# Two graph-attention layers: r stored by target tile, and the neighbour lists' parts regrouped so that an adjacency load has rows of 4 KB

## The chip, the cores and the metric

One of the eight cores of a Trainium2 chip runs the whole program in one launch. The metric is device time in microseconds (us): the median of several executions of the same program, less being better. The profile shows one further execution, recorded instruction by instruction, with its own time.

## The reference: what is computed

`x` is 4096 nodes by 256 features, `adj` a 4096 x 4096 matrix of 0 and 1 in int32 (a node pair is joined with a probability of about 0.8%, and each node is joined to itself). Two attention layers run one after the other over the same matrix. Cut to what matters:

```python
# layer 0: 8 heads of 128; layer 1: 4 heads of 64, with W and a of its own
Wh  = einsum('nf,hfd->hnd', x, W_heads)
s1, s2 = Wh @ a1, Wh @ a2                       # one number per node and head
e   = leaky_relu(s1[target] + s2[source], 0.2)  # for each pair
att = softmax(where(adj > 0, e, -inf), over sources)
hp  = att @ Wh
# layer 0: x = layernorm(x + elu(hp) @ W_out + b_out)
# layer 1: x = layernorm(x + hp), the result
```

`exp(leaky_relu(a + b))` is the larger of two products, each of a factor of the target and a factor of the source. So the kernel needs, per node and head, one factor of the target, called `r`, and two of the source, called `c` and `q`.

## The kernel before, in words

**Layer 0 is sparse.** The 4096 targets form 32 tiles of 128, and each tile 8 groups of 16, so there are 256 groups. For a group the kernel lists all nodes that are joined to any of its 16 targets, and fetches the table rows of these nodes by an indirect DMA (a gather, line 858): four gathers of 128 rows for a group. A table row holds the 256 features, the source's factors, and one 16-bit word per group of the phase, which tells which targets the source is joined to. VectorE makes the weights from `r` and the row's factors (lines 964 to 978), TensorE multiplies weights and rows (line 986), and the sums are turned into features, projected and normalised (from line 1025 on).

**The lists come from bit words.** Work runs in 8 phases of 4 tiles (512 targets). For each phase the adjacency rows of its targets are loaded in 16 pieces of 128 targets by 1024 sources (`load`, line 538, its DMA at line 548), turned into bf16 (`convert`), and multiplied on TensorE by powers of two (`count`), which leaves one word per source and group. The words lie in a tile of 128 partitions by 1024 columns: partition block `q` of 32 partitions (one per group) and its 1024 columns are the list's part `q`, which is a quarter of the nodes. Before the change part `q` is the nodes 1024q to 1024q + 1023. The words arrive in two halves of 512 columns, [...]and so a piece for one half takes, for two of the parts, 512 sources each: two runs of 2 KB in a row of the adjacency. From the words and the node's number (`node`, written once at line 458) VectorE picks the largest eight at a time (`take`), at most 160 in each part. The words also go into the table's rows by way of four transposes and copies (`bits`, `note`), and `publish` (line 676) writes them to the table in DRAM.

**r goes through DRAM.** The factor `r` of the targets is made in 4 chunks of 8 tiles (`Scores.chunk`), transposed to one row of 128 values per head and tile, and stored in the DRAM tensor `r_d` (`store`, line 423, its DMA at line 426). Before the change `r_d` of a chunk is laid out as head, tile, target. `Near` (line 909) then loads, for each target tile, the 8 heads' rows of that tile into all 128 partitions (`rb`, line 916): eight runs of 512 B for each partition, 1024 runs in all. Right behind it on the same queue `Near` loads the tile's own table rows (`own`, line 920). Layer 1 has its own `r_d`; it reads, for one head, the 8 tiles of a chunk in a run of 4 KB (line 1272).

**What sets the order.** The layer 0 code stands in one order written out by hand (`tc.manual_schedule`), and each engine works through its own list in that order:
- SyncE's queue (SP) issues nearly all plain loads: the adjacency pieces, `rb`, `own`, `y`, the weights, and `table` stores of later phases. An instruction that waits there holds all that stand behind it.
- ScalarE (ACT) has a queue too: half of the first phase's adjacency pieces, the layer 0 weights `w0T` (line 774), the stores of `r_d`, and the four `table` stores of the first phase (line 678).
- GpSimd (POOL) issues the gathers. `gather` (line 852) runs 5 groups ahead, with 6 buffers.
- Adjacency pieces of later phases have 3 buffers, and a piece is converted two pieces after it is loaded. A planner (`pick`, `busy`, `spare`) spreads VectorE's list work over the groups; its costs are not touched by the change.

**The opening** (`opening`, line 766) is all that stands before the first gather: the first phase's adjacency, the factors, the first phase's lists, the table's first copy, and the second phase's adjacency. After it the loop over the 256 groups begins (line 1189). **Layer 1** (from line 1378) is dense: it loads the transposed adjacency in pieces with rows of 4 KB (line 1279), makes weights on VectorE and multiplies on TensorE.

If a list overflows or a factor leaves its range, a flag at the end (line 1448) starts a slow general path. It does not run with these inputs.

Of the kernel before, what the change touches and what calls it, by code (L numbers as in the profile page):

```python
# [9 lines left out]
F32 = mybir.dt.float32  # L10
BF16 = mybir.dt.bfloat16
I32 = mybir.dt.int32
# [6 lines left out]
P = 128  # L19
# [243 lines left out]
def fast_path(  # L263
# [72 lines left out]
    class Scores:  # L336
# [3 lines left out]
        def __init__(self, n, H, pj, cj):  # L340
            self.n, self.H, self.pj, self.cj = n, H, pj, cj
            self.v = small.tile([P, KC, 2, H], F32, tag="v", name=f"v_{n}", bufs=1)
            self.d = const.tile([P, NT, H], F32, name=f"d_{n}")
            self.mx = const.tile([P, H], F32, name=f"mx_{n}")
            self.r_d = dram.tile([NCH, H, CT, P], F32, name=f"r_d_{n}")

        def weights(self, a_sb, wT_sb):
            pv = ps_m.tile([P, KC, 2, self.H], F32, tag="m", name=f"pv_{self.n}")
# [11 lines left out]
        def chunk(self, k, src):  # L360

            n, H = self.n, self.H
            held = {}

            def scores():
                ps = held["ps"] = ps_0.tile([P, CT, 2, H], F32, tag="o1", name=f"ps_{n}_{k}")
                for t in range(CT):
                    for c in range(KC):
                        nc.tensor.matmul(  # L369
                            ps[:, t],  # L370
                            src[:, c, ts(k * CT + t, P)],
                            self.v[:, c],
                            start=(c == 0),
                            stop=(c == KC - 1),
                        )

            def pull():
                pc = held["pc"] = small.tile(
                    [P, CT, 2, H], F32, tag="pc", name=f"pc_{n}_{k}", bufs=2
                )  # L380
                nc.vector.tensor_copy(pc, held["ps"])
                if k == 0:
                    ext = small.tile([P, H], F32, tag="ext", name=f"ext_{n}", bufs=1)
                    nc.vector.tensor_reduce(
                        ext, pc.rearrange("p t a h -> p a h t")[:, 1], AX.X, ALU.max
                    )
                    held["pe"] = ps_m.tile([H, P], F32, tag="m", name=f"pe_{n}")
                    nc.tensor.transpose(held["pe"], ext, ident)

            def top():  # L390

                if k == 0:
                    top = small.tile([H, 1], F32, tag="top", name=f"top_{n}", bufs=1)
                    nc.vector.tensor_reduce(top, held["pe"], AX.X, ALU.max)
                    dg = small.tile([H, H], F32, tag="dg", name=f"dg_{n}", bufs=1)
                    nc.vector.tensor_scalar(dg, ident[0:H, 0:H], top, None, ALU.mult)
                    held["pm"] = ps_m.tile([P, H], F32, tag="m", name=f"pm_{n}")
                    nc.tensor.matmul(held["pm"], ones[0:H, :], dg, start=True, stop=True)

            def factors():  # L400
                if k == 0:
                    nc.vector.tensor_copy(self.mx, held["pm"])
                pc = held["pc"]
                mx = self.mx.unsqueeze(1).to_broadcast([P, CT, H])
                r = held["r"] = small.tile([P, H, CT], F32, tag="r", name=f"r_{n}_{k}", bufs=1)
                rt = r.rearrange("p h t -> p t h")
                nc.vector.tensor_tensor(rt, pc[:, :, 0], mx, ALU.add)
                nc.vector.tensor_scalar(r, r, SPREAD, None, ALU.min)
                nc.scalar.activation(r, r, AF.Exp, scale=1.0 - SLOPE)
                d = self.d[:, ts(k, CT), :]  # L410
                nc.vector.tensor_tensor(d, pc[:, :, 1], mx, ALU.subtract)
                dc = small.tile([P, CT, H], F32, tag="dc", name=f"dc_{n}_{k}", bufs=1)
                nc.vector.tensor_scalar(dc, d, -SPREAD, RISE, ALU.max, ALU.min)
                nc.scalar.activation(
                    self.pj[:, ts(k, CT), :], dc, AF.Exp, scale=SLOPE - (0.0 if n == 0 else 1.0)
                )
                nc.scalar.activation(self.cj[:, ts(k, CT), :], dc, AF.Exp)

            def turn():
                held["pr"] = ps_m.tile([H * CT, P], F32, tag="m", name=f"pr_{n}_{k}")  # L420
                nc.tensor.transpose(held["pr"], held["r"].rearrange("p h t -> p (h t)"), ident)

            def store():
                row = small.tile([H * CT, P], F32, tag="row", name=f"row_{n}_{k}", bufs=1)
                nc.vector.tensor_copy(row, held["pr"])
                nc.scalar.dma_start(self.r_d[k].rearrange("h t p -> (h t) p"), row)

            return [scores, pull, top, factors, turn, store]

# [26 lines left out]
    node = keep0.tile([P, QN], mybir.dt.uint16, name="node")  # L456
    for q in range(NQ0):
        nc.gpsimd.iota(
            node[ts(q, GP), :], pattern=[[-1, QN]], base=N - q * QN, channel_multiplier=0
        )  # L460
    one = const.tile([P, T], I32, name="one")
    nc.gpsimd.memset(one, 1)
# [67 lines left out]
    def words_of(s):  # L530

        pw = []
        raw, bins = {}, {}
        HN = QN // 2
        NW = PT * NQ0
        PQ = NQ0 // 2

        def load(m):

            k, t, q = m // (PT * PQ), m // PQ % PT, m % PQ  # L540
            if s == 0:
                G = gpool.tile([P, NB, RW], F32, tag="G", name=f"Ga_{m}")
                v = G.rearrange("p b w -> p (b w)")[:, 0 : 2 * HN].bitcast(I32)
                raw[m] = v.rearrange("p (a n) -> p a n", a=2)
            else:
                raw[m] = apool.tile([P, 2, HN], I32, tag="aq", name=f"aq_{s}_{m}")
            queue = nc.scalar if s == 0 and m % 2 else nc.sync
            queue.dma_start(
                raw[m],
                adj[ts(s * PT + t, P), :].rearrange("p (q k n) -> p k q n", k=2, n=HN)[  # L550
                    :, k, ts(q, 2)
                ],
            )

        def convert(m):
            mb = two.tile([P, 2, HN], BF16, tag="mb", name=f"mb_{s}_{m}", bufs=2)
            if s == 0:
                nc.vector.tensor_scalar(mb, raw.pop(m), 0.0, 0.5, ALU.is_gt, ALU.subtract)
            else:
                nc.scalar.activation(mb, raw.pop(m), AF.Sign, bias=half[:, 0:1])  # L560
            bins[m] = mb

        def count(m):


            k, t, q = m // (PT * PQ), m // PQ % PT, m % PQ
            if t + q == 0:
                pw.append(ps_0.tile([P, HN], F32, tag="o2", name=f"pw_{s}_{k}", bufs=1))
            mb = bins.pop(m)
            for a in range(2):  # L570
                r = ts(2 * q + a, GP)
                nc.tensor.matmul(  # L572
                    pw[k][r, :],
                    word[:, t, :],
                    mb[:, a],
                    start=(t == 0),
                    stop=(t == PT - 1),
                    tile_position=(0, (2 * q + a) * GP),
                    skip_group_check=True,
                )  # L580
            if t == PT - 1 and q == PQ - 1:
                if k == 0:
                    words[s] = two.tile([P, QN], F32, tag="ws", name=f"ws_{s}", bufs=2)

                nc.scalar.activation(
                    words[s][:, ts(k, HN)],
                    pw[k],
                    AF.Identity,
                    bias=half[:, 1:2],
                    scale=1.0 if s == 0 else 0.5,  # L590
                )

        lag = 5 if s == 0 else 2

        def piece(m):
            for f, mm in ((load, m), (convert, m - lag), (count, m - lag - 1)):
                if 0 <= mm < NW:
                    f(mm)

        return [lambda m=m: piece(m) for m in range(NW + lag + 1)]  # L600

    def lists_of(s):
# [15 lines left out]

        def others():

            j0 = s * PT * P
            o = ws[ts(j0 // QN, GP), ds(j0 % QN, PT * P)]
            nc.vector.tensor_tensor(o, o, other[ts(j0 // QN, GP), :], ALU.mult)

        def halve(k):

# [41 lines left out]
            held[k] = pt  # L668

        def note(k):  # L670
            o = tail[:, :, WD - F :].bitcast(I32).rearrange("p (q k) g -> p k q g", q=NQ0)
            pt = held.pop(k)
            for q in range(NQ0):
                nc.scalar.copy(o[:, ts(k, 4), q], pt[:, :, q])

        def publish(k, n):
            t = NT // n
# [231 lines left out]
    class Near:  # L909
# [3 lines left out]
        def __init__(self, i):  # L913
            self.i = i
            self.rb = two.tile([P, H0, P], F32, tag="rb", name=f"rb_0_{i}")
            nc.sync.dma_start(
                self.rb, sc0.r_d[i // CT, :, i % CT, :].unsqueeze(0).to_broadcast([P, H0, P])
            )
            self.rows = two.tile([P, RW], F32, tag="own", name=f"own_{i}")
            nc.sync.dma_start(self.rows, table[i // PT % 2][ts(i, P), :])  # L920
# [575 lines left out]
```

## Time and profile before

| what | value |
|---|---|
| median of 3 runs | 2341.47 us (2330.23 to 2343.05) |
| the profiled execution | 2615.83 us, of which its span 2614.0 us |
| opening, span 0 to 124 us | first gather issued at 123.33 us |
| layer 0's loop, 124 to 1860 us | POOL is busy for 1051 us of it |
| layer 1, 1860 to 2614 us | PE is busy for 726 us of it |
| DMA packets | 229,332, of which 33,664 of 512 B and 32,768 of 2 KB |
| mean granted TensorE clock | 0.900 |

The page of the profile has six parts: busy time by engine; the span in 40 slices; the DMA queues; the chain of work that ended last, followed back from the end; groups of instructions by line and form, with the idle time before them; and the DMA issues. Engines are PE (TensorE), PEld (its weight loads), DVE (VectorE), ACT, POOL and SP. A waiting time is put down to the one that ended it. Queue q1 is SP's, q10 ACT's, and q0 that of POOL's gathers. The profiled execution took 274 us longer than the median of the runs, so a stretch of it can't be taken for a stretch of a timed run without a second thought.

### The profile page before, as it was taken

The numbers are of one execution on the slowest core, as the hardware profiler recorded it, in microseconds if no ns is written. First come the engines' busy times: TensorE is split into PE (matmuls) and PEld (weight loads), VectorE is DVE, ScalarE is ACT, GpSimd is POOL, SyncE is SP. The second block draws the span as 40 slices with busy tenths as digits, with TensorE's granted clock in tenths as the row PEclk, the third lists the DMA queues.
The fourth block names the chain that finished last, engine by engine and source line by source line (L and its number), as shares of the span: only waits on it lengthen the run. The fifth ranks groups of instructions, "written<-read, shape, count | busy, mean of one in ns | idle before, by whom it ended". The sixth has DMA issues, their size and how long they took to land.

```text
span 2614.0 us, 35749 instructions
## 1 busy us (share of the span) xinstructions
PE 2171.0 (83%) x12585; PEld 1302.0 (50%) x12585; DVE 1994.5 (76%) x4347; ACT 804.0 (31%) x1569; POOL 1087.6 (42%) x1158
## 2 busy tenths in 40 slices
PE   4357877887788887788878778878899999999997
PEld 3234555565565555556545556656553432324433
DVE  4358687777777787767767886666599799999997
ACT  1313323322322322332332222312343444434332
POOL 1066566565665666656556666664000000010110
PEclk9978888888888898888889888888999999999998
DMA  7968465556636746755554644543676566666653
GB/s 258 237 161 240 133 152 181 153 141 185 182 110 145 218 139 158 197 144 151 158 168 123 138 121 115 131 124 83 227 245 192 173 203 200 214 202 222 185 180 98
DMA packets 229332, 443.54 MB, mean 170 GB/s; under 512 B 60820, under 2 KB 125463, under 8 KB 229143
## 3 DMA queue, kind: packets, MB, share of 16 engines
q1 hardware_dynamic: 168790, 264.94, 34.3%
q0 software_dynamic: 52224, 169.97, 23.7%
q10 hardware_dynamic: 8128, 6.25, 0.8%
q8 instruction: 101, 1.65, 0.2%
q14 instruction: 89, 0.72, 0.1%
HBM read 426.04 MB, written 23.40 MB: 172 GB/s over the span
## 4 chain that ended last, share of the span: by engine, by line
PE 63%; another core or an unknown queue 12%; DVE 8%; ACT 6%; DMA 5%; issue 5%; POOL 1%; SPq 0%; DVEq 0%; ACTq 0%; POOLq 0%
PE po L986 26%; PE po L1298 16%; PE po L1310 8%; PE ph L1046 3%; PE py L1069 3%; PE pa L1017 2%; DMA G<-table,ids 2%; ACT mb L560 1%; ACT ag L1010 1%; ACT rb_s L885 1%; PE ps L369 1%; PE pw L572 1%; DVE e L964 1%; DVE e L970 1%
## 5 line engine op out<-in xcount | busy, mean ns | idle before, releaser
L858 POOL DMA_INDIRECT G<-table,ids x1024 | 979.2, 956 | 618.6 <-issue 262.5
L1408 DVE SCALAR_TENSOR_TENSOR e<-rb,pj,mb 128x1024 f32<-128x1024 f32 x512 | 631.0, 1279 | 48.3 <-PE po L1310 24.4
L986 PE MATMUL po<-G,e 128*128 128x257 f32 x2048 | 618.5, 454 | 20.5 <-DVE e L978 9.0
L1298 PE MATMUL po<-e,wh 128*32 128x512 f32 x4096 | 623.9, 594 | 8.5 <-DVE e L1408 5.8
L986 PEld LDWEIGHTS po<-G,e 128*128 128x128 f32 x2048 | 432.3, 222 | 187.7 <-issue 54.8
L1310 PE MATMUL po<-e,cj 128*32 128x512 f32 x2048 | 457.6, 592 | 0.0
L1280 ACT ACTIVATE mb<-aq 128x1024 bf16<-128x1024 int32 x256 | 271.0, 1058 | 411.8 <-DVE e L1408 348.2
L986 PE MATMUL po<-own,eo 128*128 128x257 f32 x512 | 185.8, 448 | 246.1 <-ACT ag L1010 191.4
L1020 ACT COPY aT<-pa 128x256 f32<-128x256 f32 x256 | 94.9, 371 | 872.7 <-remote 307.0
L1298 PEld LDWEIGHTS po<-e,wh 128*32 128x32 f32 x4096 | 202.8, 110 | 281.2 <-issue 174.5
L446 POOL TENSOR_TENSOR rstd<-rstd,neg_half 128x1 f32<-128x1 f32 x32 | 28.4, 891 | 726.7 <-DVE rstd L445 537.1
L986 PEld LDWEIGHTS po<-own,eo 128*128 128x128 f32 x512 | 85.9, 211 | 269.7 <-ACT ag L1010 207.0
L986 PE MATMUL po<-Gs,e_s 32*128 32x257 f32 x512 | 202.8, 479 | 18.3 <-DVE e_s L907 18.3
L1310 PEld LDWEIGHTS po<-e,cj 128*32 128x32 f32 x2048 | 127.5, 110 | 137.8 <-issue 103.9
L964 DVE TENSOR_TENSOR e<-rb,side 128x512 f32<-128x512 f32 x256 | 175.8, 687 | 9.3 <-issue 0.3
L970 DVE TENSOR_TENSOR e<-e,side 128x512 f32<-128x512 f32 x256 | 175.8, 687 | 8.9
L978 DVE TENSOR_TENSOR e<-e,side 128x512 f32<-128x512 f32 x256 | 175.7, 686 | 8.8
L1005 DVE TENSOR_SCALAR rd_all<-po 128x1 f32<-128x1 f32 x256 | 38.6, 151 | 180.7 <-PE po L986 131.7
L1046 PE MATMUL ph<-aT,w_sb 128*128 128x128 f32 x1024 | 154.7, 296 | 7.9 <-issue 7.5
L1046 PEld LDWEIGHTS ph<-aT,w_sb 128*128 128x128 f32 x1024 | 143.1, 208 | 23.8 <-issue 18.0
L1010 ACT ACTIVATE ag<-po,rd_all 128x256 f32<-128x256 f32 x256 | 120.5, 471 | 96.5 <-DVE rd_all L1006 55.0
L986 PEld LDWEIGHTS po<-Gs,e_s 32*128 32x128 f32 x512 | 84.5, 206 | 117.6 <-issue 98.6
(158 smaller groups left out, 2089.6 us busy)
## 6 DMA issues: line engine op xcount, KB each, us to landing
aq<-in_adjT SPq DMA_DIRECT2D x256, 512.0 KB
aq<-in_adj SPq DMA_DIRECT2D x112, 512.0 KB
rb<-r_d SPq DMA_DIRECT2D x48, 512.0 KB
G<-table,ids POOLq DMA_INDIRECT x1024
table<-in_x SPq DMA_DIRECT2D x8, 1024.0 KB
table<-tail SPq DMA_DIRECT2D x56, 98.0 KB
own<-table SPq DMA_DIRECT2D x32, 152.5 KB
Ga<-in_adj SPq DMA_DIRECT2D x8, 512.0 KB
```

Of the source, the lines that this page charges most:

```text
L858: nc.gpsimd.indirect_dma_start(out=G[:, b, :], out_offset=None, in_=table[s % 2][:, :], in_offset=bass.IndirectOffsetOnAxis(ap=lists[s][:, ...
L964: nc.vector.tensor_tensor(e, rb[:, :, ts(n % GT, T)].unsqueeze(1).to_broadcast(sh), f_p[:, :, 0:H0].unsqueeze(3).to_broadcast(sh), ALU.mult,)
L970: nc.vector.tensor_tensor(e, e, f_p[:, :, H0:].unsqueeze(3).to_broadcast(sh), ALU.max)
L978: nc.vector.tensor_tensor(e, e, nb_p.unsqueeze(2).to_broadcast(sh), ALU.mult)
L986: nc.tensor.matmul(po, w.rearrange("p h t -> p (h t)"), v[:, 0 : F + 1], start=first, **kw)
L1010: nc.scalar.activation(ag, po[:, 0:F], AF.Copy, scale=rd_all[:, n : n + 1])
L1020: nc.scalar.copy(aT[:, :, :, ts(n % GT, T)], pt)
L1046: nc.tensor.matmul(phs[k][:, hh, :], w_sb[:, c, ts(h, D0)], aT[:, c, h, :], start=(c == 0), stop=(c == KC - 1),)
L1280: nc.scalar.activation(mb, aq, AF.Relu, scale=OPEN)
L1298: nc.tensor.matmul(po[q][ts(b, DQ), :], wh[:, j, k, d : d + DQ], es[k][:, ts(q, HB)], start=(j == 0), stop=(j == NT - 1), tile_position=(0 ...
L1310: nc.tensor.matmul(po[NQ][r0 : r0 + DQ, :], sc1.cj[:, j, 2 * g + k : 2 * g + k + 1].to_broadcast([P, DQ]), es[k][:, ts(q, HB)], start=(j = ...
L1408: nc.vector.scalar_tensor_tensor(e, rb[k], sc1.pj[:, j, h : h + 1], mb, ALU.max, ALU.min)
```

## The change

Three things change together, and nothing else.

1. `r_d` of layer 0 is laid out as tile, head, target. `store` writes its 64 rows of 512 B to permuted places, and `Near` reads one run of 4 KB for each partition, 128 runs in all where it was 1024.
2. Part `q` of a list is now two runs of 512 nodes, those from 512q on and those from 2048 + 512q on. The two runs that a piece of the adjacency takes now lie side by side in the matrix, and a piece has one run of 4 KB for each partition where it had two of 2 KB. 128 pieces are loaded in all.
3. `node`, `others` and `note` follow the new numbering, with the same number of instructions and the same shapes.

The built program has the same instructions in the same order on each engine, with the same waits. What differs is the form of three DMAs: the adjacency pieces are 128x1024 where they were 128x2x512, the `rb` loads 128x1024 where they were 128x8x128, and the `r_d` stores 8x8x128 where they were 64x128.

```diff
-            self.r_d = dram.tile([NCH, H, CT, P], F32, name=f"r_d_{n}")
+
+            sh = [NCH, CT, H, P] if n == 0 else [NCH, H, CT, P]
+            self.r_d = dram.tile(sh, F32, name=f"r_d_{n}")
...
-                nc.scalar.dma_start(self.r_d[k].rearrange("h t p -> (h t) p"), row)
+                r_d = self.r_d[k] if n else self.r_d[k].rearrange("t h p -> h t p")
+                nc.scalar.dma_start(r_d, row)
...
-            node[ts(q, GP), :], pattern=[[-1, QN]], base=N - q * QN, channel_multiplier=0
+            node[ts(q, GP), :],
+            pattern=[[-N // 2, 2], [-1, QN // 2]],
+            base=N - q * (QN // 2),
+            channel_multiplier=0,
...
-                adj[ts(s * PT + t, P), :].rearrange("p (q k n) -> p k q n", k=2, n=HN)[
-                    :, k, ts(q, 2)
-                ],
+                adj[ts(s * PT + t, P), ts(k * PQ + q, 2 * HN)].rearrange(
+                    "p (a n) -> p a n", a=2
+                ),
...
-            j0 = s * PT * P
-            o = ws[ts(j0 // QN, GP), ds(j0 % QN, PT * P)]
-            nc.vector.tensor_tensor(o, o, other[ts(j0 // QN, GP), :], ALU.mult)
+            k, q = divmod(s, NQ0)
+            o = ws[ts(q, GP), ts(k, PT * P)]
+            nc.vector.tensor_tensor(o, o, other[ts(q, GP), :], ALU.mult)
...
-            o = tail[:, :, WD - F :].bitcast(I32).rearrange("p (q k) g -> p k q g", q=NQ0)
+            o = tail[:, :, WD - F :].bitcast(I32)
+            o = o.rearrange("p (k q m) g -> p k q m g", q=NQ0, m=4)[:, k]
             pt = held.pop(k)
             for q in range(NQ0):
-                nc.scalar.copy(o[:, ts(k, 4), q], pt[:, :, q])
+                nc.scalar.copy(o[:, q], pt[:, :, q])
...
-                self.rb, sc0.r_d[i // CT, :, i % CT, :].unsqueeze(0).to_broadcast([P, H0, P])
+                self.rb, sc0.r_d[i // CT, i % CT].unsqueeze(0).to_broadcast([P, H0, P])
```

## The prediction, made before the changed kernel ran

> **What bounds the kernel now.** I read first the stretches, then who waits in layer 0, then the opening instruction by instruction, since the change touches DMAs alone. Busy time of each engine in three stretches (length, then busy us and number of instructions of PE, PEld, DVE, ACT, POOL, then TensorE's clock, DMA share and GB/s):
>
> ```profile
> 0.00:124.00 124.00, 57.30 (x266) 41.68 (x266) 54.90 (x161) 27.98 (x51) 7.76 (x23) 1.00 0.80 248
> 124.00:1860.00 1736.00, 1387.46 (x5930) 974.39 (x5931) 1257.59 (x3400) 479.76 (x1160) 1051.42 (x1104) 0.85 0.56 151
> 1860.00:2614.00 754.00, 726.20 (x6391) 285.98 (x6389) 682.00 (x786) 296.26 (x358) 28.45 (x32) 0.99 0.62 199
> ```
>
> No engine is busy for half of the opening, but the DMA engines are for 80%: it is bound by transfers. In the loop DMA is busy for 56% only. Layer 1 is bound by PE and DVE, and the change doesn't touch it. From the page, the chain's shares and the gathers' row:
>
> ```profile
> PE 63%; another core or an unknown queue 12%; DVE 8%; ACT 6%; DMA 5%; issue 5%; POOL 1%; SPq 0%; DVEq 0%; ACTq 0%; POOLq 0%
> ...
> L858 POOL DMA_INDIRECT G<-table,ids x1024 | 979.2, 956 | 618.6 <-issue 262.5
> ```
>
> A gather takes 0.95 us and 0.30 us of issue, so 1.25 us; 1,088 of them (64 are `Gs`) need 1,360 us. The profiled execution took 274 us more than the median (2615.83 - 2341.47), and the chain's 12% without a releaser is about 314 us. I found these waits all in the loop, with TensorE's semaphores arriving late in bursts and the clock at half after them, and I take them for a mark of this execution. A timed loop is then about 1736 - 274 = 1,462 us; less the 49 us from the last gather (1811) to 1860, gathers are issued over some 1,413 us, of which POOL needs 1,360. So in the timed runs POOL sets the pace of the loop, with about 53 us of stall, and the end moves with the first gather. What precedes it, on SP's queue and on ACT's (start, length of issue, instruction):
>
> ```profile
> 100.92 0.46 SPq L916 DMA_DIRECT2D rb<-r_d  x1
> 101.44 1.21 SPq L920 DMA_DIRECT2D own<-table  x1
> 102.69 0.97 SPq L1178 DMA_DIRECT2D w_sb<-in_w0f  x1
> 103.71 2.15 SPq L1179 DMA_DIRECT2D wo_sb<-in_w_out  x1
> 105.90 1.97 SPq L1180 DMA_DIRECT2D b_sb<-in_b_out  x1
> 107.91 3.82 SPq L916 DMA_DIRECT2D rb<-r_d  x1
> 112.98 3.17 SPq L920 DMA_DIRECT2D own<-table  x1
> ```
>
> ```profile
> 108.49 1.49 ACTq L678 DMA_DIRECT2D table<-tail  x1
> ...
> 112.99 2.46 ACT L885 COPY rb_s<-rb 32x128 f32<-32x128 f32 x8 [2.22 <-DMA rb<-r_d]
> ```
>
> The first `rb` lands 12 us after its issue, and all behind it on SP's queue waits. POOL starts at 123.33. The wait list names `own`, but the semaphore that ends POOL's wait at 122.4 is that of the last `table` store, issued by ACT at 108.49.
>
> The DMA queues while a later `rb` is loaded (620.5 to 628.5), and while layer 1 loads two of its own in 4 KB runs (1856 to 1862):
>
> ```profile
> DMA packets 1189, 1.03 MB, mean 129 GB/s; under 512 B 62, under 2 KB 1085, under 8 KB 1189
> q1 hardware_dynamic: 1039, 0.52, 28.4%
> ...
> DMA packets 454, 1.58 MB, mean 264 GB/s; under 512 B 50, under 2 KB 72, under 8 KB 454
> q1 hardware_dynamic: 447, 1.58, 95.0%
> ```
>
> 1,024 small packets keep the engines busy for 28% of 8 us, at 0.52 MB in that time; 4 KB runs move 1.58 MB in 6 us. So the small-run `rb` holds its queue for 8 to 9 us (first to last packet, 7.1 to 9.6 us in the 29 loads that I measured in the loop); in 4 KB runs at 264 GB/s, 0.52 MB is 2 us.
>
> [...] The packet records agree: median 27, 46, 84, 159 ns for 512 B, 1, 2, 4 KB, about 9 ns fixed. That alone makes an adjacency piece 5% cheaper, no more. [...]
>
> **The change part by part**, as the shift of the first gather.
> - *First phase's adjacency* (0 to 28 us, DMA saturated): 16 pieces x 256 packets x 87 ns (share 105.2% of 15 us x 16 engines over 2,902 packets, 5 to 20 us) / 16 = 22.3 us; in 4 KB, 2,048 x 165 ns / 16 = 21.1. -1.2 us.
> - *`w0T` behind it*: the chain waits for it (lands 39.9). [...] +2.3 us at most, +1.2 taken. These two cancel; both ends, -1.2 and +1.1, are kept.
> - *Second phase's adjacency* (61 to 103 us, DMA share 0.97 up to 100): 13 pieces. By the 9 ns, 13 x 0.07 = 0.9 us. Here 2 KB packets averaged about 110 ns; if the 26 ns on top of 84 are a cost for each packet, a piece goes from 1.76 to 1.47 us, 3.8 us in all. I take -2; this shortens waits for `aq` in the chain.
> - *`rb` of tiles 0 and 1*: each holds the queue 6 us less. The first one's cover is none: weights and `own` behind it move up by 6 us. The `table` store issued at 108.49 moved 880 of its 1,024 packets by 117; its last came at 122, in the slow stretch of the second `rb` and `own`. With weights and `rb` gone by 111 it should land at about 116.5: -6 us. Bounds: 0 if its tail has another cause, -10 if the weights alone held it.
> - *First gather's landing*: [...] +0.5 us (0 to 1).
> - *`rb` in the loop*, 30 more: nothing. It is issued at a tile's start and first used three groups (about 16 us) later; landing at 9 us is covered. VectorE's first use (line 937) shows no idle time in 32. Without the cover it would be 30 x 6 us.
> - *Pieces in the loop*, 96: nothing. ACT's 10.8 us of waiting for `aq` (line 560) all lie before 150 us.
> - *`r_d` stores*: [...] nothing. *`node`*: four iota take 4.05 us from 2.2 us on and are first read at 43.7; even doubled, nothing. *`note`, `others`*: same shapes and counts. No wait is added, and no instruction moves past another.
>
> Sum: 0 - 2 - 6 + 0.5 = -7.5 us, on the profiled execution 2615.8 to 2608.3. The opening is not where that execution lost its 274 us, so the same 7.5 us come off the median: 2341.5 - 7.5 = 2334.0 us, or 0.3%.
>
> **The rivals.**
> - *Nothing is gained.* The first gather waits for something else in the 61 to 124 us stretch: the lists' numbers are ready at 111.9, and POOL's wait names several DMAs. Against: those loads are ahead in the same queue. About 2341 us.
> - *The loop gains as well.* SP's queue is free 30 x 6 us longer, and part of the 53 us of POOL's stall goes: with two fifths of it, 2334 - 21 = 2313 us. For: stores to `table` and pieces share that queue. Against: POOL waits for gathers only 10.8 us.
> - *Slower.* [...] The price: 112 pieces x 8 packets on an engine x 75 ns = 67 us if all of it delays a gather that is waited for. It decides from where a gather lands later than 10 us after its issue, eight gathers back, since POOL reuses eight semaphores. With a third of it, and the opening's gain, 2334 + 22 = 2356 us. Against: 2.5 to 4 us from issue to landing in the loop's start, and POOL's small wait.
> - *The change isn't done*: the built program shows 128x1024 for both loads, so this is small and lies in the first rival.
>
> **How the numbers follow.** Chances: forecast 0.50 (2328 to 2340, its own bounds), nothing gained 0.17 (2338 to 2345), loop gains 0.21 (2300 to 2329), slower 0.12 (2347 to 2375). The range 2311 to 2351 leaves about half of each of the last two outside and holds the bounds of the unknown costs. 0.5% is 11.7 us, about what a measurement of this kernel can tell from no change: faster is the loop case and a fifth of the forecast, 0.31; slower 0.11; the same 0.58.
>
> **What would show it.** In the profile after: 2 KB packets gone from layer 0 and 32,768 fewer of 512 B; `rb` held by SP's queue for 2 to 3 us; the first gather at about 116 instead of 123.33; POOL's row unchanged at 956 ns; layer 1 at 754 us. I am wrong if the first gather doesn't move, if POOL's idle time for DMA grows by more than 10 us, or if `rb` in 4 KB runs holds its queue as long as before.

## The result, and the profile after

| | median us | range, runs | profiled span |
|---|---|---|---|
| before, runs beside the change | 2336.66 | 2330.23 to 2343.05, 4 | 2614.0 |
| before, profiled once more | 2333.54 | 2325.44 to 2339.32, 20 | 2327.1 |
| after | 2301.70 | 2298.95 to 2304.78, 4 | 2303.0 |

The ratio is 0.9851 (95%: 0.9815 to 0.9887): 1.5% faster, where 0.3% was forecast (2334.0) and 2311 was the lower end of the range. Some executions, of before as of its variants, ran with a mean TensorE clock of 0.90 instead of 0.96 and took about 2600 us (the first profile of before is one, and four late experiments were), so they are compared only among themselves; readings of "before" are of its second profile unless the first is named.

Stretches of that profile of before, then of after (length; busy us and instructions of PE, PEld, DVE, ACT, POOL; clock, DMA share, GB/s). The second ends 9 us behind the last gather:

```profile
0.00:124.00 124.00, 57.59 (x266) 41.68 (x266) 55.29 (x161) 28.19 (x51) 10.53 (x26) 1.00 0.80 253
124.00:1550.00 1426.00, 1247.41 (x5805) 884.23 (x5806) 1240.55 (x3379) 481.90 (x1143) 1050.27 (x1100) 0.95 0.65 182
1550.00:2327.10 777.10, 746.88 (x6515) 304.64 (x6513) 688.15 (x808) 303.90 (x375) 29.14 (x33) 0.98 0.61 197
```

```profile
0.00:124.00 124.00, 57.70 (x266) 41.66 (x266) 55.04 (x161) 27.97 (x51) 8.20 (x23) 1.00 0.80 251
124.00:1524.00 1400.00, 1246.05 (x5806) 886.99 (x5807) 1240.69 (x3379) 482.04 (x1143) 1053.02 (x1103) 0.95 0.67 185
1524.00:2303.00 779.00, 748.58 (x6515) 304.19 (x6513) 688.22 (x808) 303.97 (x375) 29.16 (x33) 0.98 0.61 196
```

The loop is 26 us shorter (1426 to 1400) with the same work in it; layer 1 is the same. The 12% of the chain without a releaser, which the first profile of before had, are gone in both. The gathers' row (count; busy us and mean ns; idle us before them, of which issue), before and after:

```profile
L858 POOL DMA_INDIRECT G<-table,ids x1024 | 981.2, 958 | 349.9 <-issue 239.0
```

```profile
L865 POOL DMA_INDIRECT G<-table,ids x1024 | 980.4, 957 | 320.3 <-issue 236.1
```

A gather costs what it did; POOL idles 29.6 us less before them. So POOL paces the loop, as forecast, and the gain is stall (time in which POOL, ready for its next gather, has to wait) that went away. What POOL and VectorE waited for in the loop (150 to 1490 us; total, times, longest), before and after:

```profile
DVE side L963 <- DMA G<-table,ids: 65.0, 25, 6.9
POOL G L858 <- DMA G<-table,ids: 23.8, 39, 1.9
```

```profile
DVE side L970 <- DMA G<-table,ids: 30.6, 24, 3.9
POOL G L865 <- DMA G<-table,ids: 7.9, 15, 3.3
```

Gathers land earlier. The opening gave nothing back: these instructions of after answer to those shown in the prediction, and the last is the first gather.

```profile
104.16 0.43 SPq L923 DMA_DIRECT2D rb<-r_d  x1
104.64 0.42 SPq L927 DMA_DIRECT2D own<-table  x1
105.10 0.72 SPq L1185 DMA_DIRECT2D w_sb<-in_w0f  x1
...
109.41 1.67 SPq L923 DMA_DIRECT2D rb<-r_d  x1
...
112.31 0.44 ACTq L685 DMA_DIRECT2D table<-tail  x1
...
122.89 1.18 POOL L880 DMA_INDIRECT Gs<-table,ids  x1 [115.00 <-DMA table<-tail]
```

Once the first `rb` is issued, SP's queue is freed sooner, as forecast, but that first `rb` is issued 3 to 4 us later than in either profile of before (104.16 against 100.92 and 99.87), and POOL starts at 122.9; in the two profiles of before it started at 123.3 and 119.6. A first gather that doesn't move was one of the prediction's own signs of being wrong.

### The profile page after: what moved, and what is told of

The parts are those of the page before. It is cut to its first block, busy times and chain, and to the rows that moved or that the text cites. A ratio compares the mean times of both kernels' runs of the same rounds, so it can differ in the third digit from the quotient of the medians.

```text
span 2303.0 us, 35768 instructions
## 1 busy us (share of the span) xinstructions
PE 2052.3 (89%) x12585; PEld 1232.8 (54%) x12585; DVE 1984.0 (86%) x4347; ACT 814.0 (35%) x1569; POOL 1090.4 (47%) x1158
## 2 busy tenths in 40 slices
DMA packets 184244, 443.55 MB, mean 193 GB/s; under 512 B 60787, under 2 KB 92662, under 8 KB 184054
## 4 chain that ended last, share of the span: by engine, by line
PE 45%; DVE 30%; DMA 13%; POOL 5%; issue 5%; ACT 1%; SPq 1%; DVEq 0%; ACTq 0%; POOLq 0%
PE po L1305 19%; PE po L993 11%; PE po L1317 9%; DMA G<-table,ids 8%; DVE e L971 5%; DVE e L977 4%; DVE e L985 4%; POOL G L865 4%; PE py L1076 2%; DVE side L970 2%; DVE side L979 2%; DMA Gs<-table,ids 1%; DMA aq<-in_adj 1%; PE ph L1053 1%; DVE lst L655 1%
## 5 line engine op out<-in xcount | busy, mean ns | idle before, releaser
L993 PE MATMUL po<-G,e 128*128 128x257 f32 x2048 | 562.0, 421 | 83.7 <-DVE e L985 83.2
L1305 PE MATMUL po<-e,wh 128*32 128x512 f32 x4096 | 625.6, 595 | 7.8 <-DVE e L1415 4.8
L993 PEld LDWEIGHTS po<-G,e 128*128 128x128 f32 x2048 | 398.1, 205 | 231.8 <-DVE e L985 129.0
L993 PE MATMUL po<-own,eo 128*128 128x257 f32 x512 | 165.8, 406 | 56.3 <-ACT ag L1017 51.7
L993 PE MATMUL po<-Gs,e_s 32*128 32x257 f32 x512 | 181.9, 435 | 15.4 <-DVE e_s L914 15.4
L1053 PE MATMUL ph<-aT,w_sb 128*128 128x128 f32 x1024 | 146.6, 289 | 0.2 <-ACT aT L1027 0.2
L1053 PEld LDWEIGHTS ph<-aT,w_sb 128*128 128x128 f32 x1024 | 136.3, 201 | 13.7 <-issue 8.2
L566 ACT ACTIVATE mb<-aq,half 128x1024 bf16<-128x1024 int32 x112 | 128.7, 1151 | 33.8 <-DMA aq<-in_adj 15.5
L993 PEld LDWEIGHTS po<-Gs,e_s 32*128 32x128 f32 x512 | 76.4, 186 | 103.1 <-issue 87.0
L1076 PE MATMUL py<-wo_sb,hT 128*128 128x256 f32 x512 | 125.9, 389 | 0.0
```

The source lines that it names most:

```text
L993: nc.tensor.matmul(po, w.rearrange("p h t -> p (h t)"), v[:, 0 : F + 1], start=first, **kw)
L1053: nc.tensor.matmul(phs[k][:, hh, :], w_sb[:, c, ts(h, D0)], aT[:, c, h, :], start=(c == 0), stop=(c == KC - 1),)
L1076: nc.tensor.matmul(pys[0], hT[:, h, :], wo_sb[:, h, :], start=False, stop=(h == H0 - 1))
L1305: nc.tensor.matmul(po[q][ts(b, DQ), :], wh[:, j, k, d : d + DQ], es[k][:, ts(q, HB)], start=(j == 0), stop=(j == NT - 1), tile_position=(0 ...
```

## The experiments

**Each half alone.** Theories at this point: R, the gain comes from the `rb` loads, which hold SP's queue for a shorter time; A, from the adjacency's longer rows; S, from both. `r_only` has the three edits of `r_d` alone, `adj_only` the others. `before_again` is before, unchanged.

> Only r's layout is changed (the rb loads in 4 KB runs, the r_d stores permuted); the adjacency pieces keep two runs of 2 KB. Theory R (the rb loads hold SP's queue 8 us a tile, and freeing it takes stall from the loop): nearly all of the 35 us, so about 2305 us. Theory A (the adjacency pieces' longer rows do it): within 8 us of before. Theory S (each half takes part): 2315 to 2325 us.

> Only the lists' parts are changed (adjacency pieces in rows of 4 KB, node, others and note renumbered); the rb loads keep 1024 runs of 512 B. Theory R: within 8 us of before. Theory A: about 2302 us. Theory S: 2315 to 2325 us.

Measured: r alone 2293.51 us, ratio 0.9814 (0.9791 to 0.9836); adjacency alone 2339.16 us, 1.0033 (1.0022 to 1.0044); before again 2333.54, 0.9998 (0.9988 to 1.0008). So r is the whole gain, and the adjacency's half costs a third of a per cent. Taking from the traces the gathers' gaps beyond 0.30 us of issue, POOL stalls for 48.7 us before, 11.8 with r alone, 57.9 with the adjacency alone, 19.4 after. r takes off 37 us, 2 to 6 us in each of the eight phases: a loop effect, not one of the opening. Of before's stall 44.6 us lie in the 16 us behind the issue of one of the loop's 30 `rb` loads, where less than a third of the gathers are issued; with r alone 6.2 us lie there.

**What the slow `rb` does to gathers.** The prediction looked at SP's queue while an `rb` was loaded. Here is the stretch 804.5 to 810 us of before, 1.6 us behind the issue of an `rb`, then 795.4 to 800.9 of after, also 1.6 us behind one (queue: packets, MB, share of 16 engines; the last line gives the gathers issued and their median us to landing):

```profile
DMA packets 833, 0.43 MB, mean 78 GB/s; under 512 B 2, under 2 KB 833, under 8 KB 833
...
q1 hardware_dynamic: 833, 0.43, 32.6%
...
G<-table,ids POOLq DMA_INDIRECT x5, 6.9
```

```profile
DMA packets 638, 1.46 MB, mean 265 GB/s; under 512 B 122, under 2 KB 378, under 8 KB 638
...
q0 software_dynamic: 210, 0.66, 41.3%
q1 hardware_dynamic: 428, 0.80, 39.6%
...
G<-table,ids POOLq DMA_INDIRECT x5, 3.1
```

Five gathers are issued in each. Before, there is no q0 line at all: for 5.5 us not one packet of a gather moves, though the engines are busy for only a third. From the packet records, 24 of the loop's 30 `rb` loads are followed by over 3 us without a gather's packet (122 us in all), after the change none. By the semaphores' updates, gathers issued within 2 us after an `rb` land after 10.7 us in the median (5.5 after the change), those far from any `rb` after 3.2 in both. POOL's gathers use eight semaphores in turn (111 to 118 in the records), and in after none of the 544 gathers whose landing the trace has in full has the eighth behind it issued sooner than 0.26 us after that landing. With 0.95 us for a gather and 0.30 of issue, POOL so waits, by estimate, once one takes longer than 8 x 1.25 = 10 us to land: 37 of these 46 gathers land later before, none of 48 after. What shuts them out? Theory G: the number of small packets. Its tests:

```diff
 r_512         sh = [NCH, CT, H, P + 4]          # 16 B behind each head: 1024 runs of 512 B
 r_1k          sh = [NCH, CT, H // 2, 2 * P + 4] # behind two heads: 512 runs of 1 KB
```
```diff
 r_more_256, r_more_2k: r_only, and for i > 1 in Near
+                more = keep0.tile([P, H0, P // 2 + 1], F32, tag="more", name=f"more_{i}")
+                # part: four heads of r as eight rows of 256 B; r_more_2k without the "+ 1"
+                nc.scalar.dma_start(more[:, :, 0 : P // 2], part.unsqueeze(0).to_broadcast(...))
```

> r stored by target tile as in the change, the adjacency as before, but with 16 B of padding behind each head's 512 B, so that the rb load goes back to 1024 runs of 512 B, now 528 B apart instead of 4 KB apart. Theory G (while the DMA engines work through the 1024 small packets of an rb load, no packet of a gather is moved, so gathers land late and POOL stalls): as before the change, 2325 to 2340 us, ratio 0.996 to 1.003; in the loop about 45 us of POOL's stall and some 24 of 30 rb loads with over 3 us without a gather's packet. Rival L (it is the place of the rows in DRAM, 4 KB apart, that is slow): 2288 to 2300 us, ratio 0.98, stall about 12 us.

> The same with padding behind each pair of heads: 512 runs of 1 KB for an rb load; each of the four stores of r becomes four, on ACT's queue in the opening, which may cost the opening 1 to 3 us. Theory G with a limit: the shut-out took 5.0 us for 783 packets, so 512 packets give about 3.3 us; a gather then lands about 6.5 us after its issue, less than the 10 us (8 gathers of 1.25 us) from which POOL has to wait, so most of the gain stays: 2293 to 2303 us, stall in the loop 12 to 20 us. Rival (the loss grows in proportion to the packets): half of the gain, 2310 to 2318 us, stall about 30 us.

> r in 4 KB runs as in the change, the adjacency as before, and for each tile from the third on a further load on ACT's queue that nobody reads: 4 heads of r, 256 KB, in 1024 runs of 256 B. Neither rb nor SP's queue is touched. Theory G: the gathers are shut out again for 5 to 6 us for each, so most of the gain is lost: 2320 to 2340 us, stall in the loop 35 to 60 us. Rival Q (what stood behind the slow rb on SP's queue came late) and rival U (rb itself came late): 2291 to 2300 us, stall 12 to 18 us.

> The control for the one before: the same further load of 256 KB on ACT's queue at the same places, in 128 runs of 2 KB. All theories: 2291 to 2300 us, ratio about 0.982. If it is slower than that by as much as the one with runs of 256 B, the cost lies in the extra bytes or in ACT's instruction, and not in the number of packets.

Measured: 2290.62 (0.9835), 2287.51 (0.9823), 2291.13 (0.9843) and 2290.91 us (0.9836), all intervals between 0.979 and 0.987, stall 11.4 to 13.2 us. Theory G falls: 1024 packets of 512 B for `rb`, or 1024 more of 256 B, cost nothing. What `r_512` doesn't share with before is the form of r's stores and where the eight rows lie: 528 B apart and not 4096. So rival L stood, and became theory P: the distance in the DRAM. `pitch_4k` keeps the new stores and brings the distance back. One number was changed, the padding behind each head's row:

```diff
 pitch_4k      sh = [NCH, CT, H, 1024]   # floats from one head's row to the next: 4096 B
 pitch_4608    sh = [NCH, CT, H, 1152]
 pitch_2k      sh = [NCH, CT, H, 512]
```
```diff
 r_more_p4k: the further load takes eight rows of x, 4 KB apart
+                part = x.rearrange("(i h c) f -> i h c f", h=H0, c=4)[i, :, 0, 0 : P // 2]
```

> r stored by target tile, the adjacency as before, and each head's 512 B padded to 4 KB: the rb load has 1024 runs of 512 B as in the padded run before, but 4096 B apart as before the change. Theory P (the eight rows of an rb load lie a power of two apart, [...]and the reads of gathers wait behind them): as before the change, 2322 to 2340 us, ratio 0.996 to 1.003; loop stall about 45 us; rb lands after some 10 us. If it was the order in r's layout or its stores and not the distance: 2285 to 2297 us, ratio 0.983.

> The same with 4608 B between the rows. Theory P: 2285 to 2300 us, ratio 0.983, no gap of over 3 us in the gathers' packets after most rb loads. Rival W (what is slow is that the rows are spread over 32 KB[...], and not the power of two): as with 4096 B, 2322 to 2340 us.

> The same with 2048 B between the rows. Theory P: [...] in part slower, 2293 to 2325 us; I take 2305. Rival W: 2290 to 2300 us[...].

> r in 4 KB runs, the adjacency as before, and a further load on ACT's queue that nobody reads, for each tile from the third on, in 1024 runs of 256 B as in the earlier one, but of eight rows of x that lie 4 KB apart. Theory P with the gathers as its victims: rb and SP's queue are left alone, and still the gathers land late: 2315 to 2340 us, loop stall 30 to 55 us, against 2291 us of the run with the same packets from one place. Rivals Q and U (SP's queue, or rb itself, late): 2288 to 2297 us.

| rows apart | median us | ratio (95%) | POOL stall | `rb`, first to last packet, median |
|---|---|---|---|---|
| before, 4096 B | 2334.75 | 1 | 48.7 | 8.6 us |
| 4096 B | 2327.98 | 0.9968 (0.9958 to 0.9977) | 45.2 | 8.5 |
| 4608 B | 2292.62 | 0.9818 (0.9795 to 0.9842) | 18.4 | 3.5 |
| 2048 B | 2293.31 | 0.9826 (0.9802 to 0.9850) | 13.2 | 5.0 |
| 528 B | 2290.62 | 0.9835 (0.9810 to 0.9859) | 13.2 | 4.0 |
| 512 B (4 KB runs) | 2293.51 | 0.9814 (0.9791 to 0.9836) | 11.8 | 3.2 |

(The stall of before is from its second profile, of another batch.) The same view of 5.5 us that begin 1.5 us behind the issue of an `rb`, with 4096 B and then with 4608 B between the rows:

```profile
q1 hardware_dynamic: 874, 0.45, 40.4%
q0 software_dynamic: 10, 0.01, 1.3%
...
G<-table,ids POOLq DMA_INDIRECT x5, 6.3
```

```profile
q1 hardware_dynamic: 1230, 0.76, 46.1%
q0 software_dynamic: 198, 0.64, 35.2%
...
G<-table,ids POOLq DMA_INDIRECT x5, 3.1
```

The `rb` loads have the same packets and much the same spread (32 and 36 KB); 512 B more of distance bring the gathers back. So the distance carries the loss, and the packets' number, the order of r and rival W (the spread) fall; the 0.3% by which the padded 4096 B stay below before is not explained. Of the gathers issued within 2 us after an `rb`, 28 of 44 land later than 10 us at 4096 B and none at 4608, 2048 or 528 B. 2048 B slow the `rb` itself (5.0 us), but these gathers land after 6.9 us in the median, and no time is lost: the 2305 us taken for it was a miss. That it is a power of two that matters, as theory P has it, and not for instance every multiple of 4096 B, was not tested. In `r_more_p4k` (2317.91 us, 0.9932, 0.9907 to 0.9957) neither `rb` nor SP's queue is touched, and the waits for gathers are back, against those of `r_more_256`, which issues as many packets at the same points of the program (stall 36.2 against 11.8 us):

```profile
DVE side L969 <- DMA G<-table,ids: 48.8, 21, 7.8
POOL G L860 <- DMA G<-table,ids: 31.4, 46, 3.3
```

```profile
DVE side L971 <- DMA G<-table,ids: 18.8, 15, 4.1
POOL G L860 <- DMA G<-table,ids: 7.2, 23, 0.5
```

So the gathers are the victims, and the late `rb` or SP's queue are not needed for the loss: theory R had the right half of the change and the wrong carrier. The further load has half of an `rb`'s bytes and gives back 25 of the 42 us between before and `pitch_4608` beside it.

**Why the adjacency's half costs.** Candidates: the longer packets, with which `w0T` lands at 41.6 us and not at 39.8 as with r alone (A1), or the new numbering (A2). `after_2k` is after with 16 B of padding in the middle of an SBUF row, hence packets of 2 KB (200,628 packets in all in its profile, 184,244 after); `after_open2k` has it in the first two phases only. `r_w0T` is r alone with the loads of `w0T` six pieces earlier (`m == 9`).

```diff
+                aq = apool.tile([P, 2, HN + 4], I32, tag="aq", name=f"aq_{s}_{m}")
+                raw[m] = aq[:, :, 0:HN]
```

> The changed kernel, but the SBUF tile of an adjacency piece has 16 B of padding in the middle of each row, so that a piece comes in runs of 2 KB again; the new parts of the lists stay. Theory A1 (the longer packets cost[...]): as with r alone, 2286 to 2296 us, first gather at about 119.6 instead of 122.9. Rival A2 (the new order of the nodes in the lists costs, by other rows gathered together or by the copies into the table's rows): 2297 to 2306 us, first gather still about 123.

> The same, but runs of 2 KB only for the pieces of the first two phases, which the opening loads; the 96 pieces of the later phases keep runs of 4 KB. Theory A1 in the opening: as the one before, 2286 to 2296 us. If the cost comes from the loop's pieces: 2296 to 2306 us. Rival A2: as after the change, 2297 to 2306 us.

> r in runs of 4 KB, the adjacency as before, and the weights w0T issued on ACT's queue ahead of the last three pieces of the first phase that this queue loads instead of behind them. In the profile of r alone the chain of the opening runs through w0T, which lands at 39.8; if it lands some 6 us earlier and the first words not over 3 us later, the first gather moves from 119.6 to 114 to 117 and the end with it: 2282 to 2290 us. If other loads (xT, the second phase's pieces) set the first gather: 2290 to 2295 us.

Measured: 2302.55 us (0.9858, 0.9841 to 0.9875), 2302.43 (0.9863, 0.9848 to 0.9879) and 2296.05 (0.9835, 0.9820 to 0.9850). A1 falls: with short packets `w0T` lands at 40.0, as with r alone, and the time is that of after. Moving `w0T` gains nothing either, where 2282 to 2290 us were expected: the last piece of the first phase now lands at 35.6 us instead of 26.6, and the first gather comes at 121.4. The stretch 60 to 104 us, where the second phase's pieces set the pace, in r alone and in `after_2k`:

```profile
60.00:104.00 44.00, 26.84 (x130) 21.10 (x130) 19.46 (x67) 18.63 (x23) 0.00 (x0) 1.00 0.94 243
```

```profile
60.00:104.00 44.00, 26.50 (x129) 21.24 (x130) 17.79 (x60) 17.27 (x22) 0.00 (x0) 1.00 0.92 228
```

Busy as much, but 228 GB/s instead of 243. That suggests A3: the pieces' places. A new piece takes one block of 4 KB from each of 128 rows that lie 16 KB apart; an old one took half of each of two blocks. The places were exchanged without the numbering, and another grouping of the blocks was tried.

```diff
 after_old_places / r_new_places: the old load in after / the new load in r_only; `others` follows
 order2: in after
-                adj[ts(s * PT + t, P), ts(k * PQ + q, 2 * HN)].rearrange(
+                adj[ts(s * PT + t, P), ts(2 * q + k, 2 * HN)].rearrange(
```

> The changed kernel with its new numbering of the nodes, its copies and its r, but each adjacency piece is read from the places of before (two runs of 2 KB, 4 KB apart, in each row), and the mask of the own targets follows them. The columns are so taken for other nodes, and the layers of another graph of the same density are computed; the work is the same. Theory A3 (the pieces' places in the DRAM cost: with the new ones the second phase's pieces move 236 GB/s from 62 to 104 us, also in packets of 2 KB, against 252 with the old ones): the cost of the adjacency's half is gone, 2286 to 2297 us, first gather at 117 to 120. Rival A2 (the new numbering costs in the lists, the copies or the gathers): 2299 to 2306 us, first gather at 122 to 123.

> The converse: r by target tile, the numbering of before, but the pieces read from the new places, in runs of 4 KB; again the layers of another graph are computed, with the same work. Theory A3: 2299 to 2306 us, first gather at 122 to 124. Rival A2: 2286 to 2297 us.

> The changed kernel with the lists' parts grouped in another way: a piece has one run of 4 KB as after the change, but the first half of the pieces takes the first and third 1024 columns, not the first and second, and the parts, the mask and the copies follow. Theory A3 in the form that two neighbouring blocks of 4 KB in rows 16 KB apart crowd more than others do: some of the 0.35% comes back, 2290 to 2300 us. If any run of 4 KB in rows 16 KB apart costs the same, or under rival A2: 2299 to 2306 us.

> The changed kernel with its pieces read from the places of before, once more, since the chip of the last three granted TensorE a mean clock of 0.90, as in the first profile of before, and there TensorE and not POOL paced the loop. Theory A3 where TensorE has a clock of 0.96: 2286 to 2297 us against 2330 to 2340 of before, ratio 0.982, first gather at 117 to 120, and POOL's stall in the first phase about 2 us instead of 9.8. Rival A2: 2299 to 2306 us, ratio 0.986, first gather at 122 to 123. On a chip with a clock of 0.90: no difference from before, with the first gather at 117 to 120 as in the run before.

TensorE's mean clock was 0.90 in all four, and in the runs of before beside them (2602.22 us for the first three, 2598.03 for the last): 2606.47 (0.9991, 0.9970 to 1.0013), 2610.39 (1.0032, 1.0005 to 1.0058), 2607.17 (1.0020, 1.0001 to 1.0039) and 2599.49 (1.0012, 0.9991 to 1.0034). The times can't decide between A2 and A3, but the opening, where the clock is 1.00 in all of them, can. The same stretch in `after_old_places` and `r_new_places`:

```profile
60.00:104.00 44.00, 26.13 (x127) 20.88 (x128) 19.30 (x67) 18.48 (x23) 0.00 (x0) 1.00 0.93 242
```

```profile
60.00:104.00 44.00, 26.06 (x126) 21.92 (x127) 18.09 (x61) 15.89 (x23) 0.00 (x0) 1.00 0.89 218
```

The rate goes with the places and not with the numbering: 242 GB/s, and 246 in `after_old_again`, against 218, 215 (`order2`) and 220 (after). So does the first gather: 118.7 and 118.2 us with the old places in the changed kernel, 124.4 with the new ones in the other, 126.0 in `order2`; with r's rows at any distance but 4096 B, all profiles with the old places have it at 117.0 to 119.7 (`r_w0T`, with its other order, at 121.4), those with the new ones at 120.6 to 126.0. At 4096 B the gap is small: 119.6 to 123.3 against 123.8 in `adj_only`. In the opening A3 holds, and the other grouping of 4 KB blocks does no better. That these 3 to 4 us and POOL's stall in the first phase (9.8 us after, 2.1 with r alone) make up the 8 us of the medians (2301.70 - 2293.51) fits by size, but that the stall comes from the places is not shown: in profiles with the old places it is 4.4 (`r_512`) and 7.0 us (`pitch_4608`) too, and in `after_open2k` 6.7. So the cause of the whole third of a per cent stays open.

In the executions with a mean clock of 0.90 the loop is held by something else. The chain's shares in `after_old_places`, and its gathers' row:

```profile
PE 65%; another core or an unknown queue 11%; ACT 7%; DVE 7%; issue 5%; DMA 3%; POOL 2%; ACTq 0%; DVEq 0%; POOLq 0%
...
L865 POOL DMA_INDIRECT G<-table,ids x1024 | 981.3, 958 | 621.0 <-issue 263.5
```

There POOL idles for 621 us, as in the first profile of before, and r's half, the 1.9% elsewhere, is worth nothing (0.9991 in `after_old_places`). The lower clock follows what makes these executions long and is not shown to be a cause of its own. In the five profiles of this kind the waits without a releaser are 34 to 38 pauses, 285 to 319 us in all, about what was lost, and the other profiles have none. Of 178 pauses 165 begin at full clock, and behind 156 of these the clock then falls to half, some 9 us after the pause began, as the prediction had read it in the first profile of before. TensorE's busy time grows by 119 us only (2051.9 to 2171.0 in before). What makes the pauses stays open.

## Why the prediction was wrong, by its own steps

- *What bounds the loop*: right. POOL paces it in the timed runs; a stall of 53 us was worked out, 48.7 measured.
- *"`rb` in the loop, 30 more: nothing"*: this step failed; it was worth 37 us. It asked only who reads `rb`, and that cover held. It didn't ask who else was in the DMA at the time: the gathers. The stretch shown there (620.5 to 628.5 us) held the answer, though not in the lines shown: of its 150 packets of gathers, 4 start by 620.6, none for the next 5 us, and 146 after 625.6. In the 5.5 us of before shown above q1 moves 833 packets and q0 none. The 10 us for a gather's landing stood in the rival that ended slower. I had set it against the new packets, when the old ones were already beyond it.
- *"POOL waits for gathers only 10.8 us"*: read in a profile in which most of POOL's idle time, 618.6 us, had other causes. In the second profile of before it is 23.8 us, and VectorE waits 65.0 for gathers besides.
- *The rival "the loop gains as well"* (0.21, 2313 us): the right place and sign, the wrong carrier (SP's queue) and little more than half the size (21 of 37 us). That its range, 2300 to 2329, holds the measured 2301.70 is in part luck: the 7.5 us that it counted in the opening did not come.
- *The 512 B packets as the reason for 8 to 9 us*: wrong. At 528 B of distance as many take 4.0 us.
- *`rb` of tiles 0 and 1, -6 us*: about -2, with a scatter as large. With the pieces at their old places and a clock of 0.96, the first gather comes at 117.0 to 119.7 in the eight profiles with near or padded rows, and at 119.6 and 120.9 in the two with 4096 B (123.3 in the first profile of before). `own` and the weights did move up, yet the last `table` store took 12.6 us to land before (107.0 to 119.6) and 10.6 after.
- *The adjacency's pieces, -3.2 us*: +3.3 instead in the profiles (119.6 to 122.9). The per-packet saving was right (2 x 84 - 159 = 9 ns, by the medians), but from 62 to 104 us the packet's mean is 246 ns in 4 KB after, against 112 in 2 KB before (120 with r alone, 123 in `after_2k`), so nothing is saved for the same bytes; and at the new places the stretch moves fewer GB/s. *`w0T`* +1.2: +1.8, within what was worked out, and not what decided. The +1.2, the +0.5 us of the first gather's landing and the third of 67 us in the rival that ended slower were my estimates. With packets of 4 KB `w0T` lands at 41.6 us, with 2 KB at the same places (`after_2k`) at 40.0; how the queues share the DMA engines was not shown.
- *Pieces in the loop, copies, mask, `node`: nothing*: nothing was seen of them from the second phase on (stall 1.2 to 1.8 us for each phase, as with r alone).

The loss is seen here at 4 KB, for eight rows that are read 128 times each, and 512 B of padding are enough (2327.98 us at 4096 B, 2292.62 at 4608). What in the DRAM makes it is not shown.

## What to carry to other kernels

Before a transfer is called covered, look at what the other queues move while it runs: here q0 vanished from the DMA table for 5.5 us in which five gathers were issued, with the engines busy for 32.6%, and 44.6 of the 48.7 us of stall lay behind loads like that one. When many partitions read the same few DRAM rows, try those rows at another distance: contiguous is simplest (2293.51 us here), and a padding did as well (2290.62 at 528 B, 2292.62 at 4608 B). And read the bound from an execution like the timed ones: in those with the pauses the same edit was worth nothing (0.9991 against 0.9814).

## What was not expected of the hardware

- Eight rows 4096 B apart, read by 128 partitions: 8.6 us from first to last packet and the gathers' reads shut out for about 5 us, at 33% busy engines (both in before); at 4608 B 3.5 us and no gap of over 3 us.
- Loads of one 4 KB block from each of 128 rows 16 KB apart: 215 to 228 GB/s in the stretch from 60 to 104 us, in packets of 2 KB (228) as of 4 KB (220), against 241 to 249 for two half blocks (231 and 236 in `r_w0T` and `r_1k`, which issue other DMAs in the opening).
- Executions of one kernel, before, differ by 11% (medians of 2334.75 and 2602.22 us in two batches). The longer ones have a mean TensorE clock of 0.90 instead of 0.96, and 11 to 12% of the chain in waits that end without a releaser; the pauses come first, and the clock falls behind them.
